# Scores of a cross-attention kernel: from 32-row tiles of TensorE to 64 x 64 tiles

## The chip, the cores and the metric

The kernel runs on one core of a Trainium2 chip. The metric is the device time of one execution, in microseconds (us). The engines have short names in the profile: PE is TensorE's matmuls, PEld its weight loads, DVE is VectorE, ACT is ScalarE, POOL is GpSimd and SP is SyncE, which issues most DMAs.

## What is computed

The reference is a cross-attention with a second, small attention beside it, all in float32 (16 batches, 100 queries of 640, 718 keys of 384, 8 heads of 80):

```python
query = hidden_states @ Wq
keyt = enc @ Wk
valt = enc @ Wv
hs = _mha(query, keyt, valt)          # softmax(q k^T / sqrt(80)) v, 8 heads
ca_q1 = jnp.einsum('btc,th->bch', ca, Wq_ca)
ca_q1 = ca_q1[:, indices, :]
ca_hs1 = _mha(ca_q1, residual, residual)
ca_q2 = ca_hs1 @ Wq
ca_hs2 = _mha(ca_q2, ca @ Wk_ca, ca @ Wv_ca)
out = (hs + ca_hs2) @ Wout + b_out + residual
```

The change is about the product of queries and keys in the first `_mha`: for each batch and head, 718 keys by 100 queries, over 80 rows (the head's width).

## The kernel before

The 718 keys of a batch are cut into six chunks of 120 or 119 (`KC`, `KN` = 120). Scores are computed with the keys on the output's partitions: the stationary operand is a piece of the keys `kT` (head rows by 120 keys), the moving operand a piece of the queries `qp` or `qz` (head rows by 100 queries). Exponentials `st` then serve as stationary operand of the weighted values (L1419), whose outputs are 64 and 36 queries on two column tiles.

A head has 80 rows, which do not divide the 128 rows of TensorE's array. The kernel permutes the columns of `Wq` and `Wk` so that each head's first 64 rows lie in chunks 0 to 3 of `kT` and `qp`, and the last 16 rows of all eight heads together in chunk 4 (`qz` for the queries). Before the change the first 64 rows of a head stand as two halves of 32 rows, in the same quarter of the partitions, in two chunks. So `scores` issues for each key chunk four matmuls for each of five row chunks, one in each group of 32 rows (`RG` = 4), and these four write to four banks. A head's score is the sum of two halves and of the last 16 rows. In chunk 4 a group of 32 rows holds two heads; `qz` keeps the queries of each with the other's rows masked, so these matmuls stream 200 columns instead of 100.

A batch has three groups (`g` = 0, 1, 2) of two key chunks each. `scores(b, g, tiles)` issues 40 matmuls in four banks of PSUM, and ScalarE copies them to `st`: in two copies (L629) for groups 0 and 2, which share the double-bank pool `ps2`, in four copies (L623) for group 1, which takes its banks from `psk` and `ps1`. The eight banks are all in use, so group 2 waits for the copies of group 0.

The batches follow each other in an order written out by hand (`tc.manual_schedule`, from L1199): three groups of scores, softmax2 of the second attention (`z_ps`, L788, four column tiles), its next products (`y_ps`, L736), then the products that make the next batch's keys and this batch's values (L432, L463, L557) while DVE, ScalarE and GpSimd work on the softmax, then the weighted values (`a_ps`, L1419), and the next batch. Every second batch also computes the queries of the next two batches (`q_ps`, L533). In front of the loop the weights are loaded and permuted: `load_packed` (L69) loads the transposed Wk, in nine DMAs of SP's queue, and DVE copies Wq into its permuted place (L1148 and L1155).

Of the kernel before, what the change touches and what calls it, by code (L numbers as in the profile page):

```python
# [14 lines left out]
B, S, H = 16, 100, 640  # L15
NH, D = 8, 80
CAD, T = 384, 4
SK = 722 - T
P = 128
HC = H // P  # L20
# [3 lines left out]
KN = KT // 2  # L24

KC = [(u, j) for j in range(2) for u in range(3)]
# [27 lines left out]
for h in range(NH):  # L54
    lo = h * D
    while lo < (h + 1) * D:
        c = lo // P
        hi = min((h + 1) * D, (c + 1) * P)
        PIECES.append((h, c, lo - h * D, lo - c * P, hi - lo))
        lo = hi  # L60
# [5 lines left out]
RG = 4  # L66


def load_packed(load, to, w):  # L69

    rows = w.rearrange("(r u k) n -> r u k n", r=RG, u=2)
    for r, u in [(r, u) for r in range(RG) for u in range(2)]:
        load(
            out=to[32 * r : 32 * r + 32, 2 * u : 2 * u + 2],
            in_=rows[r, u, :64].rearrange("(j p) n -> p j n", j=2),
        )
    load(out=to[:, 4], in_=w.rearrange("(h k) n -> h k n", h=NH)[:, 64:])

# [45 lines left out]
def kernel(  # L126
# [18 lines left out]
    nc = tc.nc  # L145
# [14 lines left out]
    def pair(name):  # L160
        tile = ps2.tile([P, 2, 512], F32, tag="ps2", name=name)
        return tile
# [21 lines left out]
    def scores_tile(name):  # L184
        return main.tile([P, 2, ROWS], F32, tag="st", name=name, bufs=NP)
# [28 lines left out]
    def load_enc(b):  # L214
        enc = enc_tile(f"enc_{b}"), None
        for u, lo, hi in ((0, 0, 3), (1, 1, 3), (2, 0, 2)):
            at = A_RAW[u, lo]
            nc.sync.dma_start(
                out=enc[0][:, at : at + hi - lo],
                in_=enct[b][:, lo:hi, u * (KT - 1) : u * (KT - 1) + KT],  # L220
            )
        return enc

    def load_rest(b, enc):
        if b == 1:
            room = hsT_tile("rest_1").rearrange("p c s -> p (c s)")
            rest = room[:, : len(A_REST) * KT].rearrange("p (i k) -> p i k", k=KT)
        else:
            rest = rest_tile(f"rest_{b}")
        for (u, c), i in A_REST.items():  # L230
            nc.sync.dma_start(
                out=rest[:, i], in_=enct[b][:, c, u * (KT - 1) : u * (KT - 1) + KT]
            )
        return enc[0], rest
# [6 lines left out]
    def a_form(enc, f):  # L241
        return enc[0][:, A_AT[f]]
# [10 lines left out]
    wq_sb = const.tile([P, HC, H], F32, name="wq_sb")  # L253
    kT = const.tile([P, HC, 3, KT], F32, name="kT")
# [22 lines left out]
    for g in range(2):  # L277
        for c in range(CC):
            nc.scalar.dma_start(
                out=wv_sb[:, 2 * c + g],  # L280
                in_=wv[c * P : (c + 1) * P, g * (H // 2) : (g + 1) * (H // 2)],
# [15 lines left out]
    ca_0 = small.tile([S, T, S], F32, tag="ca", name="ca_0")  # L297
    in_order(nc.sync.dma_start(out=ca_0, in_=cas[0].unsqueeze(0).to_broadcast([S, T, S])))
    load_packed(
        lambda **ends: in_order(nc.sync.dma_start(**ends)), wkt_sb[:, :, :CAD], wkt  # L300
    )
    halves = [t[:, u] for t in [scores_tile(f"wq_{i}") for i in range(NP)] for u in range(2)]
    room = halves.pop()
    wq_in = [t[:, :H] for t in halves]
# [19 lines left out]
    for h, c, r, s, k in PIECES:  # L324
        nc.gpsimd.dma_start(
            out=m2[s : s + k, c, h - HEADS[c][0], :T],
            in_=wqcat[h * D + r : h * D + r + k, :],
# [4 lines left out]
    for c in range(HC):  # L332
        first = c * P - HEADS[c][0] * D
        nc.gpsimd.affine_select(
            out=hmask[:, c], in_=hmask[:, c], compare_op=ALU.is_ge, fill=0.0,
# [3 lines left out]
            out=hmask[:, c], in_=hmask[:, c], compare_op=ALU.is_ge, fill=0.0,  # L339
# [68 lines left out]
    class Values(Blocks):  # L408
# [17 lines left out]
        def product(self, at, f, first, last):  # L426
            for bank in "AB":
                if self.opened[bank] is at and bank in self.fresh:
                    first = True
                    self.fresh.discard(bank)  # L430
            for j in range(2):
                nc.tensor.matmul(  # L432
                    at[0][j][:KN, : H // 2],
                    a_form(self.enc, f)[:, j * KN : (j + 1) * KN],
                    wv_there.get(f, wv_sb[:, W_AT[f]]),
                    start=first,
                    stop=last,
                    skip_group_check=True,
                )
# [152 lines left out]
    def scores(b, g, tiles):  # L592

        qp, qz = tiles
        name = f"s_ps_{b}_{g}"
        if g == 1:
            s_ps = [f(f"{name}_{r}") for r, f in enumerate((psumk, psumk, psum1, psum1))]
        else:
            pairs = [pair(f"{name}_{i}") for i in range(2)]
            s_ps = [pairs[r // 2][:, r % 2] for r in range(RG)]  # L600
        n = KN
        for a in range(2):
            u, j = KC[2 * g + a]
            for c in range(HC):
                for r in range(RG):
                    rows = slice(32 * r, 32 * r + 32)
                    if c < 4:
                        rhs = qp[rows, c // 2, c % 2, (b % 2) * S : (b % 2 + 1) * S]
                        lo, hi = (c // 2) * S, (c // 2 + 1) * S
                    else:  # L610
                        rhs, lo, hi = qz[rows, 0, b % 2], 0, 2 * S
                    nc.tensor.matmul(  # L612
                        s_ps[r][:n, 256 * a + lo : 256 * a + hi],
                        kT[rows, c, u, j * KN : (j + 1) * KN],
                        rhs,
                        start=(a == 0 and c == 0),
                        stop=(c == HC - 1),
                        skip_group_check=True,
                    )
        st = scores_tile(f"st_{b}_{g}")[:n]  # L620
        if g == 1:
            for r in range(RG):
                nc.scalar.copy(  # L623
                    st[:, :, 2 * r * S : 2 * (r + 1) * S],
                    s_ps[r][:n].rearrange("p (a q) -> p a q", a=2)[:, :, : 2 * S],
                )
        else:
            for i in range(2):
                nc.scalar.copy(  # L629
                    st[:, :, 4 * i * S : 4 * (i + 1) * S].rearrange(  # L630
                        "p a (r q) -> p r a q", r=2
                    ),
                    pairs[i][:n].rearrange("p r (a q) -> p r a q", a=2)[:, :, :, : 2 * S],
                )
        return st
# [80 lines left out]
    class Second:  # L716
# [87 lines left out]
        def load(self):  # L804
            self.vb = [self.piece(nc.gpsimd, t) for t in range(2)]
# [282 lines left out]
    for n in range(HC):  # L1088
        for c in range(CC):
            for lo in (0, 64):  # L1090
# [4 lines left out]
                    start=(c == 0),  # L1095
                    stop=(c == CC - 1),
                )
    k2T, at = [], 0
    for n, heads in enumerate(HEADS):
        cols = len(heads) * B * T  # L1100
# [10 lines left out]
    for c in range(HC):  # L1111
        m_ps = psum(f"m_ps_{c}")
        for n, heads in enumerate(HEADS):
# [4 lines left out]
                start=(n == 0),  # L1118
                stop=(n == HC - 1),
                skip_group_check=True,  # L1120
# [23 lines left out]

    with tc.issue_after(summed.ins):
        for c in range(HC):
            for u in range(2):
                nc.vector.tensor_copy(  # L1148
                    wq_sb[:, c, 2 * u * P : 2 * (u + 1) * P].rearrange(
                        "p (a r k) -> p a r k", a=2, r=RG  # L1150
                    ),
                    wq_in[c].rearrange("p (r k) -> p r k", r=RG)[:, :, u * D : u * D + 64]
                    .rearrange("p r (a k) -> p a r k", a=2),
                )
            nc.vector.tensor_copy(  # L1155
                wq_sb[:, c, 4 * P :].rearrange("p (h k) -> p h k", h=NH),
                wq_in[c].rearrange("p (h k) -> p h k", h=NH)[:, :, 64:],
            )
# [7 lines left out]
    for c in range(CC):  # L1166
        for n in range(2):
# [4 lines left out]
                start=(c == 0),  # L1172
                stop=(c == CC - 1),
# [3 lines left out]
    for n in range(2):  # L1177
        nc.scalar.dma_start(
            out=va_d[:, n * (H // 2) : (n + 1) * (H // 2)],
            in_=va[n * B * T : (n + 1) * B * T],  # L1180
# [10 lines left out]
    last, enc_next, second_next = None, load_rest(1, load_enc(1)), Second(1, xT)  # L1191
# [8 lines left out]
    for b in range(B):  # L1200
        p = b // 2
# [37 lines left out]
        if b == 0:  # L1239
            enc_sums(enc)  # L1240
            now.load()
            now.softmax1()
        st.append(scores(b, 0, tiles))
        if b == 0:
            now.exponentials1()
        nc.vector.tensor_tensor(most[:KN], st[0][:, 0], st[0][:, 1], ALU.max)
        st.append(scores(b, 1, tiles))
        larger(1)
        st.append(scores(b, 2, tiles))

        now.softmax2()
# [39 lines left out]
        elif b + 1 < B:  # L1291
# [68 lines left out]
            if last.b in PAIRS:  # L1360
                second.softmax1(3)
                last.project_pair()
                if last.b == max(PAIRS):
                    nc.sync.dma_start(
                        out=forms[1],
                        in_=wout[: 2 * P, H // 2 :].rearrange("(c p) n -> p c n", p=P),
# [40 lines left out]
        for g in range(2):  # L1407
# [6 lines left out]
            for h, i in order:  # L1414
# [3 lines left out]
                for lo, hi in QC:  # L1418
# [4 lines left out]
                        start=(i == 0 and h in (0, *range(4, NH))),  # L1423
                        stop=(i == len(KC) - 1),
                        skip_group_check=True,
# [6 lines left out]
            cols = slice(4 * g * D, 4 * (g + 1) * D)  # L1432
# [11 lines left out]
        last = mine  # L1444
# [55 lines left out]
```

## Time and profile before

| | |
|---|---|
| median of 3 runs | 930.88 us |
| lowest, highest | 930.83, 931.11 us |
| span of the profiled execution | 929.5 us |
| instructions in the profile | 25894 |
| PE, PEld busy | 922.4 (99%), 787.6 (85%) us |
| DVE, ACT, POOL busy | 693.2 (75%), 433.9 (47%), 678.2 (73%) us |
| granted TensorE clock | 1.000 |

The span runs from the first to the last instruction of the profiled execution. No own time of that execution is given beside its span; the timed runs are 1.3 to 1.6 us longer than it. PE and PEld overlap: the array streams one tile's columns while the next weights are loaded. A float32 matmul stands as two records on PE and two on PEld. The records' durations are latencies of single instructions, and several tiles of the array can be at work at once, so a group's pitch is read from starts and not from durations.

### The profile page before, as it was taken

To read this page: it belongs to the slowest core of one execution; us is meant where nothing else is said; L and a number is where in the kernel's file an instruction comes from. 1 tells how busy PE (TensorE), PEld (TensorE's weight loads), DVE (VectorE), ACT (ScalarE), POOL (GpSimd) and SP (SyncE) were. 2 spreads that over 40 slices of the span, in tenths; PEclk is the share of its full clock that TensorE was granted. 3 is DMA by queue.
4 is the path that set the end of the run, shared out by engine and by line. 5 is a ranking of instruction groups with operands and counts; after the bars stand their busy time and mean duration, and the time that the engine had idled before them with its cause. 6 is when DMAs were issued, how large, how long until landed. Compare 5 with 4: busy or idle time off the path is not lost.

```text
span 929.5 us, 25894 instructions
## 1 busy us (share of the span) xinstructions
PE 922.4 (99%) x11130; PEld 787.6 (85%) x11130; DVE 693.2 (75%) x1085; ACT 433.9 (47%) x836; POOL 678.2 (73%) x646
## 2 busy tenths in 40 slices
PE   9999999999999999999999999999999999999998
PEld 6998989797897979888798788988879888797966
DVE  3859895989739896685967869579873888838884
ACT  2234543736337363652726436264641737427341
POOL 5757998788938877496884968758895578956724
PEclk9999999999999999999999999999999999999999
DMA  8722022040300304031030400205030050310201
GB/s 262 264 85 77 25 66 76 7 149 2 117 17 23 105 13 120 2 103 53 28 105 3 120 36 30 75 2 154 2 103 30 2 154 2 102 45 2 82 19 41
DMA packets 49673, 62.82 MB, mean 68 GB/s; under 512 B 14072, under 2 KB 38200, under 8 KB 49560
## 3 DMA queue, kind: packets, MB, share of 16 engines
q1 hardware_dynamic: 45512, 51.49, 18.3%
q0 software_dynamic: 3024, 8.53, 3.0%
q8 instruction: 87, 1.43, 0.6%
q10 hardware_dynamic: 1024, 1.15, 0.4%
q14 instruction: 26, 0.21, 0.1%
HBM read 55.59 MB, written 5.57 MB: 66 GB/s over the span
## 4 chain that ended last, share of the span: by engine, by line
PE 97%; DVE 2%; DMA 0%; issue 0%; ACT 0%; POOL 0%; ACTq 0%; DVEq 0%
PE s_ps L612 12%; PE a_ps L1419 12%; PE v_psA L432 11%; PE v_psB L432 9%; PE kT_ps L557 8%; PE k_psA L463 7%; PE q_ps L533 7%; PE k_psB L463 6%; PE o_ps L1013 5%; PE v_psC L432 3%; PE k_psC L463 3%; PE v_psD L432 2%; PE v_psE L432 2%; PE y_ps L736 2%; PE v_ps L373 1%; PE k_psE L463 1%
## 5 line engine op out<-in xcount | busy, mean ns | idle before, releaser
L761 POOL TENSOR_TENSOR e<-ca,g 100x800 f32<-100x800 f32 x64 | 99.4, 1564 | 126.8 <-DVE most L1234 99.7
L498 POOL TENSOR_TENSOR enc<-enc 128x240 f32<-128x240 f32 x135 | 106.7, 800 | 19.7 <-DMA enc<-in_enct 12.7
L1222 DVE TENSOR_TENSOR st<-st,over 120x1600 f32<-120x1600 f32 x48 | 117.0, 2439 | 0.0
L1419 PEld LDWEIGHTS a_ps<-vs,st 120*36 120x36 f32 (+3 forms) x3072 | 109.3, 125 | 5.9 <-issue 5.8
L1419 PE MATMUL a_ps<-vs,st 120*36 120x81 f32 (+3 forms) x3072 | 112.2, 233 | 0.9 <-issue 0.9
L432 PE MATMUL v_psA<-wv_sb,enc 128*120 128x320 f32 x352 | 109.8, 434 | 0.0
L862 POOL TENSOR_TENSOR hs<-hs,hs 100x640 f32<-100x640 f32 x48 | 100.5, 2095 | 3.8
L612 PE MATMUL s_ps<-qp,kT 32*120 32x100 f32 x3072 | 97.5, 263 | 0.0
L855 POOL TENSOR_TENSOR hs<-vb,p 100x640 f32<-100x640 f32 x64 | 89.6, 1411 | 9.5 <-issue 4.7
L612 PEld LDWEIGHTS s_ps<-qp,kT 32*120 32x120 f32 x3072 | 94.7, 179 | 1.7 <-issue 0.2
L629 ACT COPY st<-s_ps 120x800 f32<-120x800 f32 x64 | 49.7, 828 | 98.1 <-PE s_ps L612 98.1
L768 POOL TENSOR_TENSOR e<-e,e 100x800 f32<-100x800 f32 x48 | 92.0, 1917 | 3.8
L432 PE MATMUL v_psB<-wv_sb,enc 128*120 128x320 f32 x296 | 91.8, 433 | 0.0
L1230 ACT ACTIVATE st<-st 120x1600 f32<-120x1600 f32 x48 | 73.9, 1539 | 32.3 <-DVE st L1222 32.1
L463 PE MATMUL k_psA<-enc,wk_sb 128*128 128x240 f32 x360 | 87.7, 366 | 0.0
L1234 DVE TENSOR_TENSOR most<-most,st 120x800 f32<-120x800 f32 x64 | 69.0, 1078 | 21.9 <-ACT st L623 20.8
L463 PEld LDWEIGHTS k_psA<-enc,wk_sb 128*128 128x128 f32 x360 | 68.3, 190 | 16.7
L432 PEld LDWEIGHTS v_psA<-wv_sb,enc 128*120 128x120 f32 x352 | 63.2, 183 | 22.6 <-DVE vs L403 0.5
L463 PE MATMUL k_psB<-enc,wk_sb 128*128 128x240 f32 x300 | 73.1, 366 | 0.1
L432 PEld LDWEIGHTS v_psB<-wv_sb,enc 128*120 128x120 f32 x296 | 54.1, 183 | 21.9 <-DVE vs L403 0.4
L928 ACT COPY hsT<-turned_hs 32x160 f32<-32x160 f32 (+7 forms) x244 | 67.7, 278 | 3.0
L533 PE MATMUL q_ps<-xT,wq_sb 128*128 128x200 f32 x400 | 69.1, 333 | 0.0
(168 smaller groups left out, 1802.9 us busy)
## 6 DMA issues: line engine op xcount, KB each, us to landing
vb<-va_d POOLq DMA_DIRECT2D x32, 250.0 KB, 3.5
vb<-va_d SPq DMA_DIRECT2D x32, 250.0 KB
enc<-in_enct SPq DMA_DIRECT2D x30, 240.0 KB
enc<-in_enct SPq DMA_DIRECT2D x15, 360.0 KB
xT<-in_xt SPq DMA_DIRECT2D x8, 500.0 KB
rest<-in_enct SPq DMA_DIRECT2D x31, 120.0 KB
xn<-in_x SPq DMA_DIRECT2D x11, 320.0 KB
out<-xn SPq DMA_DIRECT2D x11, 320.0 KB
```

Of the source, the lines that this page charges most:

```text
L432: nc.tensor.matmul(at[0][j][:KN, : H // 2], a_form(self.enc, f)[:, j * KN : (j + 1) * KN], wv_there.get(f, wv_sb[:, W_AT[f]]), start=first ...
L463: nc.tensor.matmul(at[:, i * KT : (i + 1) * KT], wk_sb[:, W_AT[f], i], a_form(self.enc, f), start=(first and i == 0), stop=last, skip_grou ...
L498: nc.gpsimd.tensor_tensor(out, left, right, op)
L533: nc.tensor.matmul(q_ps[:, : 2 * S].rearrange("p (j s) -> p j s", j=2), wq_sb[:, c, n * P : (n + 1) * P], xT[:, :, c, :], start=(c == 0), ...
L557: nc.tensor.matmul(bank[:, i * KT : (i + 1) * KT], weights[c], a_raw(enc, u, c), start=(i == 0 and c == 0), stop=(c == CC - 1), skip_group ...
L612: nc.tensor.matmul(s_ps[r][:n, 256 * a + lo : 256 * a + hi], kT[rows, c, u, j * KN : (j + 1) * KN], rhs, start=(a == 0 and c == 0), stop=( ...
L761: first = nc.gpsimd.tensor_tensor(to, self.ca[:, t, :].unsqueeze(1).to_broadcast([S, NH, S]), g[:, :, t].unsqueeze(2).to_broadcast([S, NH, ...
L768: nc.gpsimd.tensor_tensor(e, e, to, ALU.add)
L855: first = nc.gpsimd.tensor_tensor(to, self.vb[t][:S].rearrange("p (h d) -> p h d", h=NH), p2[:, :, t].unsqueeze(2).to_broadcast([S, NH, D] ...
L862: nc.gpsimd.tensor_tensor(sums, sums, to, ALU.add)
L1222: return nc.vector.tensor_tensor(st[i], st[i], top.over[:KN].unsqueeze(1).to_broadcast([KN, 2, ROWS]), ALU.subtract,)
L1419: nc.tensor.matmul(a_v[lo:hi, h % 4], st[i // 2][: KEYS[i], i % 2, h * S + lo : h * S + hi], block(i, h // 4)[: KEYS[i], h % 4], start=(i ...
```

## The change

The first 64 rows of a head now lie together, in one half of the partitions: heads 0 to 3 in rows 0 to 63 of chunks 0 to 3, heads 4 to 7 in rows 64 to 127. Their scores are computed in tiles of 64 rows by 64 columns: the 120 keys of a chunk are cut in two column tiles of 64 and 56 keys (`KH`). Four such matmuls (two halves of rows, two column tiles) take the place of the four in groups of 32 rows, with the same 100 columns streamed and the same number of matmuls, 32 in a group. The last 16 rows stay in four groups of 32 rows, 120 keys wide, 200 columns streamed, 8 matmuls in a group. They are no longer issued after each key chunk: a group issues the first rows of both chunks and then the last rows of both, and group 1 the other way round. The permutation of Wq (DVE) and the load of the transposed Wk (nine DMAs, as before) follow the new places.

```diff
+KH = [(0, 64), (64, KN)]
 def load_packed(load, to, w):
-    rows = w.rearrange("(r u k) n -> r u k n", r=RG, u=2)
-    for r, u in [(r, u) for r in range(RG) for u in range(2)]:
-        load(
-            out=to[32 * r : 32 * r + 32, 2 * u : 2 * u + 2],
-            in_=rows[r, u, :64].rearrange("(j p) n -> p j n", j=2),
-        )
-    load(out=to[:, 4], in_=w.rearrange("(h k) n -> h k n", h=NH)[:, 64:])
+    rows = w.rearrange("(h k) n -> h k n", h=NH)
+    for h in range(NH):
+        r, c = divmod(h, RG)
+        load(out=to[64 * r : 64 * r + 64, c], in_=rows[h, :64])
+    load(out=to[:, 4], in_=rows[:, 64:])
...
         n = KN
-        for a in range(2):
-            u, j = KC[2 * g + a]
-            for c in range(HC):
+        begun = set()
+        def product(at, part, w, rhs, cols, last):
+            k0, k1 = part
+            nc.tensor.matmul(
+                s_ps[at][k0:k1, cols],
+                w,
+                rhs,
+                start=not begun & {(at, k) for k in range(k0, k1, 32)},
+                stop=last,
+                skip_group_check=True,
+            )
+            begun.update((at, k) for k in range(k0, k1, 32))
+        def first_rows(last):
+            for a in range(2):
+                u, j = KC[2 * g + a]
+                for c in range(RG):
+                    rhs = qp[:, c // 2, c % 2, (b % 2) * S : (b % 2 + 1) * S]
+                    for r in range(2):
+                        h, rows = RG * r + c, slice(64 * r, 64 * r + 64)
+                        lo = 256 * a + (h % 2) * S
+                        for k0, k1 in KH:
+                            product(
+                                h // 2,
+                                (k0, k1),
+                                kT[rows, c, u, j * KN + k0 : j * KN + k1],
+                                rhs[rows],
+                                slice(lo, lo + S),
+                                last,
+                            )
+        def last_rows(last):
+            for a in range(2):
+                u, j = KC[2 * g + a]
                 for r in range(RG):
                     rows = slice(32 * r, 32 * r + 32)
-                    if c < 4:
-                        rhs = qp[rows, c // 2, c % 2, (b % 2) * S : (b % 2 + 1) * S]
-                        lo, hi = (c // 2) * S, (c // 2 + 1) * S
-                    else:
-                        rhs, lo, hi = qz[rows, 0, b % 2], 0, 2 * S
-                    nc.tensor.matmul(
-                        s_ps[r][:n, 256 * a + lo : 256 * a + hi],
-                        kT[rows, c, u, j * KN : (j + 1) * KN],
-                        rhs,
-                        start=(a == 0 and c == 0),
-                        stop=(c == HC - 1),
-                        skip_group_check=True,
+                    product(
+                        r,
+                        (0, n),
+                        kT[rows, 4, u, j * KN : (j + 1) * KN],
+                        qz[rows, 0, b % 2],
+                        slice(256 * a, 256 * a + 2 * S),
+                        last,
                     )
+        steps = (last_rows, first_rows) if g == 1 else (first_rows, last_rows)
+        for i, step in enumerate(steps):
+            step(i == 1)
...
         for c in range(HC):
-            for u in range(2):
+            for r in range(2):
                 nc.vector.tensor_copy(
-                    wq_sb[:, c, 2 * u * P : 2 * (u + 1) * P].rearrange(
-                        "p (a r k) -> p a r k", a=2, r=RG
-                    ),
-                    wq_in[c].rearrange("p (r k) -> p r k", r=RG)[:, :, u * D : u * D + 64]
-                    .rearrange("p r (a k) -> p a r k", a=2),
+                    wq_sb[:, c, : 4 * P].rearrange("p (n r k) -> p n r k", n=RG, r=2)[
+                        :, :, r
+                    ],
+                    wq_in[c].rearrange("p (r n k) -> p r n k", r=2, n=RG)[:, r, :, :64],
                 )
```

## The prediction

> **What bounds the kernel now.** I read the page first (engines, then the chain that ended last), then the list of waits of the weight loads, then the scores line by itself, then the TensorE timeline through one batch.
>
> ```profile
> span 929.5 us, 25894 instructions
> PE 922.4 (99%) x11130; PEld 787.6 (85%) x11130; DVE 693.2 (75%) x1085; ACT 433.9 (47%) x836; POOL 678.2 (73%) x646
> ...
> PE 97%; DVE 2%; DMA 0%; issue 0%; ACT 0%; POOL 0%; ACTq 0%; DVEq 0%
> PE s_ps L612 12%; PE a_ps L1419 12%; PE v_psA L432 11%; PE v_psB L432 9%; PE kT_ps L557 8%; PE k_psA L463 7%; PE q_ps L533 7%; PE k_psB L463 6%; PE o_ps L1013 5%; PE v_psC L432 3%; PE k_psC L463 3%; PE v_psD L432 2%; PE v_psE L432 2%; PE y_ps L736 2%; PE v_ps L373 1%; PE k_psE L463 1%
> ```
>
> TensorE carries 97% of the chain and is never idle for long; DVE, the next, has a quarter of the span free. What shortens TensorE's own work therefore shortens the run, as long as nothing else comes late. The scores are 12% of the chain, about 112 us, all on the path.
>
> The span is 929.5 us, the median of the runs 930.88: 1.4 us lie around the span. I work out the change of the span and take it off the median.
>
> Now the scores by themselves, and below them the weighted values (L1419), softmax2 (L788) and a value product (L432). Columns: engine, operation, out<-in, count, duration in ns (min/median/max), first and last start in us, forms; the a_ps matmuls are those of one batch, and the a_ps weight load is a row of the groups by shape (busy us, mean ns, idle before).
>
> ```profile
> L612 PEld LDWEIGHTS s_ps<-qp,kT x3072: 174/180/180, 60.0 to 885.6; 32*120 32x120 f32 x192
> L612 PE MATMUL s_ps<-qp,kT x3072: 244/263/342, 60.0 to 885.7; 32*120 32x100 f32 x192
> L612 PEld LDWEIGHTS s_ps<-qz,kT x768: 174/180/180, 60.9 to 885.8; 32*120 32x120 f32 x192
> L612 PE MATMUL s_ps<-qz,kT x768: 327/338/413, 60.9 to 886.0; 32*120 32x200 f32 x192
> L612 PEldq EVENT_SEMAPHORE  x38: 51/51/51, 98.0 to 881.0; - x38
> ...
> L1419 PE MATMUL a_ps<-vs,st x192: 231/233/284, 310.6 to 317.3; 120*64 120x81 f32 x64, 120*36 120x81 f32 x64, 119*36 119x81 f32 x32, 119*64 119x81 f32 x32
> ...
> L1419 PEld LDWEIGHTS a_ps<-vs,st 120*64 120x64 f32 x1024 | 84.5, 136 | 5.9 <-issue 5.8
> ...
> L788 PEld LDWEIGHTS z_ps<-y_sb,e x1024: 82/109/113, 67.3 to 886.8; 100*32 100x32 f32 x113, 100*4 100x4 f32 x58
> L788 PE MATMUL z_ps<-y_sb,e x1024: 191/195/218, 67.4 to 886.8; 100*32 100x33 f32 x105, 100*4 100x33 f32 x66
> ```
>
> [...] Four row groups run side by side, so four records make one set. Two prices come out of the durations:
> - **Streaming.** 200 columns take 327 ns at best, 100 take 244: 83 ns per 100 columns, 0.83 ns a column.
> - **Loading weights.** 120 columns take 180 ns, 4 columns 82 (the z row's minimum): 98 / 116 = 0.84 ns a column. So 120 columns need 100 ns, 64 need 54.
>
> The median 100-column matmul takes 263 ns, 19 more than the best one: it waits for weights, since its set streams in 83 ns while the next set's weights need 100. So 100-column sets are bound by the weight load, 200-column sets (167 ns of streaming) by the stream. The timeline of batch 5 gives the pitch (start us, duration us, engine, line, what, records):
>
> ```profile
> 310.55 6.99 PE L1419 MATMUL a_ps<-vs,st 120*64 120x81 f32 x192
> 317.47 1.10 PE L612 MATMUL s_ps<-qp,kT 32*120 32x100 f32 x32
> 318.39 0.54 PE L612 MATMUL s_ps<-qz,kT 32*120 32x200 f32 x8
> 318.75 1.00 PE L612 MATMUL s_ps<-qp,kT 32*120 32x100 f32 x32
> 319.57 0.54 PE L612 MATMUL s_ps<-qz,kT 32*120 32x200 f32 x8
> 319.92 1.00 PE L612 MATMUL s_ps<-qp,kT 32*120 32x100 f32 x32
> ...
> 322.28 1.00 PE L612 MATMUL s_ps<-qp,kT 32*120 32x100 f32 x32
> ...
> 323.46 1.00 PE L612 MATMUL s_ps<-qp,kT 32*120 32x100 f32 x32
> 324.28 0.54 PE L612 MATMUL s_ps<-qz,kT 32*120 32x200 f32 x8
> 324.75 0.75 PE L788 MATMUL z_ps<-y_sb,e 100*32 100x33 f32 x64
> 325.42 0.31 PE L736 MATMUL y_ps<-m,xT 128*100 128x72 f32 x1
> ```
>
> A half group (one key chunk) takes (323.46 - 318.75) / 4 = 1.178 us: eight sets of 100 columns and two of 200. A stream-bound product shows what a set costs beyond its streaming:
>
> ```profile
> 293.61 1.24 PE L432 MATMUL v_psC<-wv_sb,enc 128*120 128x320 f32 x4
> 294.68 1.24 PE L432 MATMUL v_psA<-wv_sb,enc 128*120 128x320 f32 x4
> ```
>
> Four records in 1.07 us are 268 to 269 ns each for 320 columns, where 0.833 x 320 = 266.7: about 2 ns more. So two 200-column sets take 2 x 169 = 338 ns, and a 100-column set (1178 - 338) / 8 = **105 ns**. A stream-bound one would take 83.3 + 2.5 = **86 ns**.
>
> **The 64-row tiles.** The new sets hold two row groups of 64 and two key column tiles of 64 and 56; still four records to a set, 100 columns streamed, 8 x 2 sets a group, 48 groups: 768 sets. Only the weight load changes, from 120 columns to 64 in the widest tile: 54 ns, under the stream. The pitch becomes 86 ns if the two column tiles of a row group load and stream side by side. No row shows two row groups and two column tiles at once. The bounds are from the nearest rows: a_ps has two column tiles of 64 and 36 over all rows and 81 columns streamed: 192 records, 96 pairs, between 310.55 and 317.47, so 6.92 / 96 = 72 ns a pair with both ends in it, against 67.5 + 2.5 of stream alone. Were their loads one after the other, 100 columns would need 84 ns. And z loads four column tiles (3 x 32 + 4 columns): 64 records, 16 sets, in 0.67 us (324.75 to 325.42, where y_ps starts), 42 ns a set, half of what 100 columns in a row need. So I take 86 ns, near a_ps: 768 x 19 ns = **14.6 us gained**. The pitch cannot go under the stream, 83 ns; the upper bound is 105 if loads queue, and the cases beyond are rivals.
>
> [...]
>
> **The switches of tile shape.** Before, a batch enters the 32-row tiles once (from a_ps or q_ps) and leaves once (to z_ps). After, the order is group 0 first rows, last rows; group 1 last rows, first rows; group 2 first rows, last rows: the last rows of groups 0 and 1 and the first rows of 1 and 2 adjoin. That makes three shape changes more in each of 16 batches. Their price: the two 200-column sets take 0.35 us from 319.57 to 319.92, where scores follow, and 0.47 from 324.28 to 324.75, where z follows, which has another shape: **0.11 us** in which the array runs empty. On top, the first weights are not hidden: the longest 100-column matmul takes 342 ns, 98 more than the best (120 columns), the longest a_ps matmul 284, 51 more than the median (64 columns). So into 32 x 120: 0.21 us; into 64 x 64: 0.16 us.
> - Added: two changes to last rows, 0.42; one back to first rows, 0.16. The entry loads 64 columns in place of 120: -0.05. Sum 0.53 us a batch, 16 batches: **8.5 us lost**.
> - Bounds: with z's small load (218 - 195 = 23 ns), the cheapest change seen costs 0.13, three of them 0.40, 5.6 us with the entry. The dearest by rows is 0.21 for each, 9.3 us.
>
> **Other edits.** Last rows keep shape, 200 columns and count: 0. The weight shuffle on DVE keeps ten copies of 256 elements:
>
> ```profile
> L1148 DVE COPY wq_sb<-wq x10: 281/288/1961, 30.2 to 35.3; 128x256 f32<-128x256 f32 x10
> ...
> L533 PE MATMUL q_ps<-xT,wq_sb x50: 332/333/437, 51.4 to 59.7; 128*128 128x200 f32 x50
> ```
>
> They end 14 us before their reader, which covers them; without cover they would cost some 3 us once. The load of Wk's transpose keeps nine DMAs on SP's queue, with as many rows of the same length; nothing moves past them: 0. In the built program z_ps waits for one more event, group 1's matmuls on its own engine, over 2 us old by then; a wait record is 51 ns in a sequencer that runs ahead: 0.
>
> **What is late next.** Group 2 reuses the banks of group 0, which ScalarE must have copied out:
>
> ```profile
> 320.19 1.55 ACT L629 COPY st<-s_ps 120x800 f32<-120x800 f32 x2 [3.51 <-PE s_ps L612]
> ```
>
> The copies end at 321.74, 1.82 us after group 0's last set (319.92). Group 1 shrinks from 2.36 us (322.28 - 319.92) to 4 x 0.169 + 16 x 0.086 + 0.16 = 2.21. The margin falls from 0.54 to 0.39 us: still free. Group 1's first copies can start four sets earlier, off the path.
>
> **Sum.** A batch now: 0.10 + 48 x 0.105 + 12 x 0.169 + 0.11 = 7.28 us, which is 317.47 to 324.75. After: loads 0.05 + 0.10 + 0.05 + 0.10, four times 0.11, 48 x 0.086, 12 x 0.169: 6.90. That is 0.38 us a batch, 6.1 us in all: span 923.4, time **924.8 us**.
>
> **Rivals.**
> 1. *The shape changes cost more than the sets save* (slower). It decides above (14.6 + 0.8) / 48 = 0.32 us a change; the dearest priced above is 0.21, but none of those goes between two row-tiled shapes. At 0.45 each: 48 x 0.26 = 12.5 us more, 937. Chance 0.03.
> 2. *A tile's load waits for matmuls in its row group*: sets of 86 + 54 = 140 ns, 768 x 35 = 27 us, with 8.5 for the switches 966. Against it: a_ps at 72 ns. Chance 0.04.
> 3. *The loads of the two column tiles of a row group queue*: 64 + 56 = 120 columns, so 105 ns as before; the gain is nothing and the entry's 0.8 goes too: about 940. Against it: a_ps and z. Chance 0.04.
> 4. *Two of the four tiles take turns streaming*: 172 ns a set, 51 us, with the switches 991. Nothing for it but that the mixture is not in the trace. Chance 0.03.
> 5. *No change*: sets near 94 ns, or switches near 0.32. Time 929 to 932.7. Chance 0.06.
>
> **How the numbers follow.** Forecast 0.80: sets 86 to 90 ns (0 to +3 us), switches 0.13 to 0.25 each (-3 to +3 us), and something below for a change that drains less than any seen. That gives 921 to 930; with the case of no change up to 930.5 and 0.5 below, the range is 920.5 to 930.5. A measurement of this kernel tells 0.2%, 1.9 us, from no change; faster means under 929.0. Slower is the sum of rivals 1 to 4.
>
> **What would show it.** After: the 64 x 64 matmuls' median within a few ns of their minimum (no wait for weights), weight loads near a_ps's 136 ns (64 columns) instead of 180, last rows unchanged, and z_ps starting 6.9 us after the first scores record instead of 7.28, in every batch. A median 19 ns or more above the minimum, or first and last rows more than 0.21 us apart at their borders, would make the steps wrong; a wait of s_ps on ScalarE would show that the banks come free too late.

## Result, and the profile after

| | before | after |
|---|---|---|
| median, four runs each on one chip | 930.86 us | 925.56 us |
| lowest, highest | 930.26, 931.11 us | 925.19, 926.35 us |
| span of the profiled execution | 929.5 us | 923.5 us |
| PE busy | 922.4 us | 916.1 us |
| PEld busy | 787.6 us | 773.0 us |

The ratio is 0.9946, with a 95% interval from 0.9931 to 0.996: the changed kernel is faster by 5.3 us. The forecast was 924.8 us, in a range from 920.5 to 930.5. The changed kernel ran twice more, beside the kernel before on those chips: 927.34 (ratio 0.9958, 0.9943 to 0.9973) and 927.32 us (0.9955, 0.9941 to 0.9968). So the gain was 5.3, 3.9 and 4.2 us in the three sets. The profiled execution took 925.19 us.

The page of the changed kernel: the span, the engines, and the chain that ended last by engine and by line.

```profile
span 923.5 us, 25899 instructions
PE 916.1 (99%) x11130; PEld 773.0 (84%) x11130; DVE 687.4 (74%) x1085; ACT 434.0 (47%) x836; POOL 685.2 (74%) x646
...
PE 96%; DVE 2%; DMA 0%; issue 0%; ACT 0%; POOL 0%; ACTq 0%; DVEq 0%
PE a_ps L1453 12%; PE s_ps L608 11%; PE v_psA L433 11%; PE v_psB L433 9%; PE kT_ps L558 8%; PE k_psA L464 8%; PE q_ps L534 7%; PE k_psB L464 6%; PE o_ps L1048 5%; PE v_psC L433 3%; PE k_psC L464 3%; PE v_psD L433 2%; PE v_psE L433 2%; PE y_ps L771 2%; PE v_ps L374 1%; PE k_psE L464 1%
```

TensorE still carries the chain (96%), with as many matmul records as before (x11130). The scores have gone from 12% to 11%.

The scores line by itself (engine, operation, out<-in, count, shortest/median/longest in ns, first and last start in us, forms):

```profile
L608 PEld LDWEIGHTS s_ps<-qp,kT x3072: 123/128/134, 60.1 to 879.0; 64*64 64x64 f32 x183, 64*56 64x56 f32 x9
L608 PE MATMUL s_ps<-qp,kT x3072: 246/246/298, 60.1 to 879.1; 64*64 64x100 f32 x183, 64*56 64x100 f32 x9
L608 PEld LDWEIGHTS s_ps<-qz,kT x768: 174/178/178, 61.6 to 879.8; 32*120 32x120 f32 x192
L608 PE MATMUL s_ps<-qz,kT x768: 327/328/425, 61.6 to 879.9; 32*120 32x200 f32 x192
```

The 100-column matmul now has its median at its minimum, 246 ns (before: 263 over 244). The 19 ns of waiting for weights are gone; the weight loads of the new tiles take 128 ns in place of 180. The longest matmuls stand at the borders: 298 - 246 = 52 ns into 64 x 64, 425 - 328 = 97 ns into 32 x 120. The prediction had 51 and 98 from other rows.

The TensorE timeline of batch 5 (start us, duration us, engine, line, what, records):

```profile
310.14 6.99 PE L1453 MATMUL a_ps<-vs,st 120*64 120x81 f32 x192
317.06 1.60 PE L608 MATMUL s_ps<-qp,kT 64*64 64x100 f32 x64
318.59 1.63 PE L608 MATMUL s_ps<-qz,kT 32*120 32x200 f32 x32
320.15 2.97 PE L608 MATMUL s_ps<-qp,kT 64*64 64x100 f32 x128
323.05 0.95 PE L608 MATMUL s_ps<-qz,kT 32*120 32x200 f32 x16
323.93 0.75 PE L823 MATMUL z_ps<-y_sb,e 100*32 100x33 f32 x64
```

The differences of the starts can be held against the prediction's sum, block by block. A block is its first load, its sets, and the 0.11 us of empty array behind it:

| block | from the prediction's numbers | measured |
|---|---|---|
| 16 sets of 64 x 64 | 0.05 + 16 x 0.086 + 0.11 = 1.54 | 318.59 - 317.06 = 1.53 |
| 8 sets of last rows | 0.10 + 8 x 0.169 + 0.11 = 1.56 | 320.15 - 318.59 = 1.56 |
| 32 sets of 64 x 64 | 0.05 + 32 x 0.086 + 0.11 = 2.91 | 323.05 - 320.15 = 2.90 |
| 4 sets of last rows | 0.10 + 4 x 0.169 + 0.11 = 0.89 | 323.93 - 323.05 = 0.88 |

Together 6.87 us from the first scores to `z_ps`, where 6.90 was said and 7.28 was before. The blocks also separate the pitch from the price of a border: 16 sets more, with the same borders, take 2.90 - 1.53 = 1.37 us, 86 ns a set. The median batch takes 6.872 us for the scores, where it took 7.276: 16 x 0.404 = 6.46 us less per execution.

**Where the rest of the 6.0 us of span is.** The other intervals between batches do not all stay. In batch 0 the time from the first `z_ps` to the first `a_ps` grew from 24.39 to 26.13 us, 1.74 lost (before, then after):

```profile
67.35 0.75 PE L788 MATMUL z_ps<-y_sb,e 100*32 100x33 f32 x64
...
91.75 2.47 PE L1419 MATMUL a_ps<-vs,st 120*64 120x81 f32 x64
```

```profile
66.93 0.75 PE L823 MATMUL z_ps<-y_sb,e 100*32 100x33 f32 x64
...
93.06 1.12 PE L1453 MATMUL a_ps<-vs,st 120*64 120x81 f32 x26
```

On the other side the profiled execution of the kernel before had an idle stretch in batch 12 (the interval between two batches' scores 48.97 us, where after it is 47.50, that is 1.06 more than the 0.4 of the scores) that the profile names only "issue"; the experiment on column tiles shows it to be a wait for instructions. In the list of waits of that kernel it is this row:

```profile
PE a_ps L1419 <- issue: 0.9, 1, 0.9
```

6.46 - 1.74 + 1.06 = 5.8; the last 0.2 us is spread over small differences.

The loss in batch 0, in the waits of TensorE's matmuls of the changed kernel (who waits, for whom, us in all, times, longest):

```profile
PE idle_ps L1114 <- DVE idle L1111: 1.1, 1, 1.1
PE k_psA L464 <- DVE kT L404: 1.1, 1, 1.1
PE y_ps L771 <- POOL m L744: 0.5, 1, 0.5
PE m_ps L1149 <- issue: 0.5, 1, 0.5
PE k_psB L464 <- DVE sm L873: 0.3, 1, 0.3
```

The second and the last row were not there before. No row names ScalarE: the banks of group 0 come free in time, as the prediction had it. VectorE's `kT` sums are late because of what stands ahead of them on VectorE, the maximum of group 2, two operations. First the kernel before, then the changed one, from the timelines of VectorE and GpSimd:

```profile
69.93 3.23 DVE L1234 TENSOR_TENSOR most<-most,st 120x800 f32<-120x800 f32 x2
70.15 4.41 POOL L761 TENSOR_TENSOR e<-ca,g 100x800 f32<-100x800 f32 x2 [0.56 <-issue]
```

```profile
69.49 4.97 DVE L1268 TENSOR_TENSOR most<-most,st 120x800 f32<-120x800 f32 x2
70.56 3.04 POOL L796 TENSOR_TENSOR e<-ca,g 100x800 f32<-100x800 f32 x2
```

And the duration of one such operation over the whole execution (shortest/median/longest ns), `most` before and after and GpSimd's product after:

```profile
L1234 DVE TENSOR_TENSOR most<-most,st x64: 981/992/2212, 66.8 to 889.3; 120x800 f32<-120x800 f32 x64
```

```profile
L1268 DVE TENSOR_TENSOR most<-most,st x64: 981/992/3956, 66.5 to 883.0; 120x800 f32<-120x800 f32 x64
L796 POOL TENSOR_TENSOR e<-ca,g x64: 1534/1539/1552, 35.5 to 845.6; 100x800 f32<-100x800 f32 x64
```

Alone `most` takes 0.99 us. Before, the longest took 2212 ns, some 1.2 more; after, 3956 ns, nearly two GpSimd products (2 x 1539) more. So it looks as if VectorE's operation stood still while GpSimd ran one product before, and two after. That was a reading of one trace; the last experiment tests it.

### The profile page after: what moved, and what is told of

Its sections match the earlier page's. It is cut to its first block, busy times and chain, and to the rows that moved or that the text cites. A ratio compares the mean times of both kernels' runs of the same rounds, so it can differ in the third digit from the quotient of the medians.

```text
span 923.5 us, 25899 instructions
## 1 busy us (share of the span) xinstructions
PE 916.1 (99%) x11130; PEld 773.0 (84%) x11130; DVE 687.4 (74%) x1085; ACT 434.0 (47%) x836; POOL 685.2 (74%) x646
## 3 DMA queue, kind: packets, MB, share of 16 engines
q8 instruction: 87, 1.43, 0.6%
## 4 chain that ended last, share of the span: by engine, by line
PE 96%; DVE 2%; DMA 0%; issue 0%; ACT 0%; POOL 0%; ACTq 0%; DVEq 0%
PE a_ps L1453 12%; PE s_ps L608 11%; PE v_psA L433 11%; PE v_psB L433 9%; PE kT_ps L558 8%; PE k_psA L464 8%; PE q_ps L534 7%; PE k_psB L464 6%; PE o_ps L1048 5%; PE v_psC L433 3%; PE k_psC L464 3%; PE v_psD L433 2%; PE v_psE L433 2%; PE y_ps L771 2%; PE v_ps L374 1%; PE k_psE L464 1%
## 5 line engine op out<-in xcount | busy, mean ns | idle before, releaser
L499 POOL TENSOR_TENSOR enc<-enc 128x240 f32<-128x240 f32 x135 | 111.0, 832 | 16.5 <-DMA enc<-in_enct 9.4
L1268 DVE TENSOR_TENSOR most<-most,st 120x800 f32<-120x800 f32 x64 | 71.2, 1113 | 15.6 <-ACT st L658 14.4
L608 PE MATMUL s_ps<-qp,kT 64*56 64x100 f32 (+1 forms) x3072 | 73.1, 248 | 0.0
L608 PEld LDWEIGHTS s_ps<-qp,kT 64*56 64x56 f32 (+1 forms) x3072 | 66.9, 130 | 5.6 <-issue 4.2
```

Of the source, the lines that this page charges most:

```text
L499: nc.gpsimd.tensor_tensor(out, left, right, op)
L608: nc.tensor.matmul(s_ps[at][k0:k1, cols], w, rhs, start=not begun & {(at, k) for k in range(k0, k1, 32)}, stop=last, skip_group_check=True,)
```

## Experiments

**The changed kernel again.** It ran in two other sets of runs, beside experiments.

> The changed kernel once more, to see whether batch 0's late products (26.1 us from z_ps to a_ps in batch 0, where the kernel before had 24.4) come again. Theory (VectorE and GpSimd collide there by the program's own timing): 26.1 us again and 925 to 926 us. Rival (chance of one execution): 24.0 to 24.6 us in batch 0, and about 924 us.

> The changed kernel, unchanged, on the same chip as the two others: 925.2 to 927.5 us, and 26.1 us from z to the weighted values in batch 0.

927.34 and 927.32 us, spans 925.7 and 925.6; the scores last 6.87 us again, in 14 and 13 of the 16 batches. Batch 0 shows 26.14 and 26.28 us from z to the weighted values: its loss is the program's own and no accident of one execution. The first time is above the 925 to 926 us expected. Its profiled execution has two idle stretches of TensorE around batch 5 that are named only "issue", and the two intervals they stand in are 1.8 us longer than in the first execution; the second run has two such stretches as well. They are of the kind that the experiment on column tiles explains.

**The price of a shape change.** The same tiles, but the last rows issued after each key chunk, so that eleven shape changes stand in a batch's scores instead of three:

```diff
-        steps = (last_rows, first_rows) if g == 1 else (first_rows, last_rows)
-        for i, step in enumerate(steps):
-            step(i == 1)
+        for a in range(2):
+            first_rows(False, [a])
+            last_rows(True, [a])
```

> The changed kernel, but the last rows are issued after each key chunk, as before the change: twelve runs of tile shapes a batch instead of four, so 11 shape changes inside a batch instead of 3. Theory (a change of shape costs 0.10 to 0.11 us of empty array plus the first weight load, 0.10 us for 120 columns and 0.05 for 64): four more changes to last rows at 0.20 and four more back at 0.16 are 1.44 us a batch, 23 us in all: about 948.6 us. Rival (the array does not run empty between two row-tiled shapes, the set pitch alone made the difference): 925 to 927 us. Rival (order does not matter but the banks come free too late): a wait of s_ps on ScalarE and a time in between.

Measured 947.04 us (946.93 to 948.5), ratio 1.0173 (1.0158 to 1.0188). The TensorE timeline of one batch, to the start of z:

```profile
322.66 0.91 PE L608 MATMUL s_ps<-qp,kT 64*64 64x100 f32 x32
323.50 0.61 PE L608 MATMUL s_ps<-qz,kT 32*120 32x200 f32 x8
324.05 0.91 PE L608 MATMUL s_ps<-qp,kT 64*64 64x100 f32 x32
...
331.04 0.75 PE L823 MATMUL z_ps<-y_sb,e 100*32 100x33 f32 x64
```

The first rows of a chunk hold 323.50 - 322.66 = 0.84 us (0.05 + 8 x 0.086 + 0.11 = 0.85), the last rows 0.55 (0.10 + 2 x 0.169 + 0.11 = 0.55). In the batches without other waits (the one shown has a short one) the scores last 8.315 us, 1.44 more than in the changed kernel: eight changes at 0.18 us each, which is the mean of the prediction's 0.21 and 0.16. The time is 1.6 us under the 948.6 expected; batch 0 does not lose its time here (24.03 us from z to the weighted values). In this order the 64-row tiles lose 16 us against the kernel before. The price of a change decides the sign, and the grouping of the steps is what pays for the tiles.

**One column tile.** The 64-row tiles with all 120 keys in one load:

```diff
-KH = [(0, 64), (64, KN)]
+KH = [(0, KN)]
```

> The changed kernel with all 120 keys in one column tile (64 rows by 120 keys; half as many matmuls for the first rows, two in a set). Theory (the gain comes from the narrower weight load): a set needs 100 ns for its weights again, pitch 105 ns instead of 86, 768 sets, and two entries a batch load 120 columns instead of 64: 14.6 + 1.5 us more than the changed kernel, about 941.5 us, slower than before the change. Rival (the gain comes from one matmul of 64 rows in place of two of 32, or from the order): 925 to 926 us.

Measured 939.13 us (938.95 to 939.97), ratio 1.0084 (1.0067 to 1.0101). The scores line, weight loads and matmuls of the first rows:

```profile
L608 PEld LDWEIGHTS s_ps<-qp,kT x1536: 176/182/182, 60.0 to 893.9; 64*120 64x120 f32 x192
L608 PE MATMUL s_ps<-qp,kT x1536: 265/265/343, 60.0 to 893.9; 64*120 64x100 f32 x192
```

The load is 182 ns again, the matmul's median 265: the 19 ns are back, with two tiles to a set and half as many loads. So with 120 columns to load, the pitch of a set is the load's, with 64 rows as with 32. The scores last 7.83 us, 0.96 longer than in the changed kernel (1.0 expected, from 48 sets at 105 instead of 86 ns and two longer first loads). The time is 2.4 us under the 941.5 expected, and again batch 0 takes 24.03 us from z to the weighted values. This is also what rival 3, loads in a queue, would have made of the change: 940 was said, 939 it is here.

**The order alone.** The old 32-row tiles, with the steps in the new order:

> The kernel before with the order of the change alone: first rows of both key chunks, then last rows of both, group 1 the other way round; tiles of 32 rows by 120 keys as before. Theory: sets cost 105 and 169 ns wherever they stand, so no change, 930 to 931.5 us. Rival (part of the gain is the order's, for example that group 1's banks are copied earlier): 925 to 929 us.

```diff
-        for a in range(2):
+        firsts = [(a, c) for a in range(2) for c in range(HC - 1)]
+        lasts = [(a, HC - 1) for a in range(2)]
+        steps = lasts + firsts if g == 1 else firsts + lasts
+        for i, (a, c) in enumerate(steps):
...
```

Measured 931.22 us (930.43 to 933.34), ratio 1.0005 (0.9996 to 1.0014); the scores last 7.276 us as before. The order by itself brings nothing; its part is to keep the shape changes few.

**Column tiles without the change of shape.** If the load bounds the 32-row tiles, two column tiles of 64 and 56 keys in the old tiles should bring the 86 ns and need no inner shape change:

```diff
-                    nc.tensor.matmul(
-                        s_ps[r][:n, 256 * a + lo : 256 * a + hi],
-                        kT[rows, c, u, j * KN : (j + 1) * KN],
...
+                    for k0, k1 in ((0, 64), (64, KN)):
+                        nc.tensor.matmul(
+                            s_ps[r][k0:k1, 256 * a + lo : 256 * a + hi],
+                            kT[rows, c, u, j * KN + k0 : j * KN + k1],
...
```

> The kernel before with one edit: every scores matmul is cut in two column tiles of 64 and 56 keys, rows in four groups of 32 as before, so eight tiles in a set, one shape for first and last rows, no change of shape inside the scores, and twice as many matmuls (80 a group). Theory (weight load of 64 columns hides under the 86 ns stream, shape changes eat 8.5 us of the change's gain): sets at 86 ns, no inner change, entry load 0.05 us shorter: 14.6 + 0.8 us less than before, about 915.5 us, ahead of both kernels. Rival (eight tiles a set are bound by the issue of 16 loads and matmuls, some 7 ns each): 112 ns a set of 100 columns, 936 us or more. Rival (loads in one row group queue): 105 ns, 930 us.

A miss: 1042.23 us (1037.9 to 1048.13), ratio 1.1196 (1.1149 to 1.1243). First lines from the list of waits of the weight loads, then the page's instruction queue (packets, MB, share) in this run and in the kernel before, then the timeline of one batch:

```profile
PEld s_ps L613 <- issue: 67.9, 46, 2.2
PEld z_ps L789 <- issue: 21.1, 25, 3.1
```

```profile
span 1036.2 us, 33574 instructions
...
q8 instruction: 117, 1.92, 0.8%
```

```profile
span 929.5 us, 25894 instructions
...
q8 instruction: 87, 1.43, 0.6%
```

```profile
357.37 0.77 PE L613 MATMUL s_ps<-qp,kT 32*64 32x100 f32 x39 [1.27 <-issue]
...
361.38 0.54 PE L613 MATMUL s_ps<-qz,kT 32*64 32x200 f32 x6 [1.81 <-issue]
```

Each batch's scores stand still for one to two microseconds several times, for nothing that another engine does. The kernel has 33574 - 25894 = 7680 instructions more, four for each of the 1920 added matmuls, and the queue moves 1.92 - 1.43 MB = 0.49 MB more, 64 bytes an instruction. Between the two gaps above lie 128 matmul records, 64 matmuls, 256 instructions: 16,384 bytes, which is the size of each packet of that queue in the trace. While scores run, such packets start 3.4 to 4.3 us apart, 3.7 in the middle (in one batch at 300.46, 304.12, 308.14, 312.16 and 316.09 us). So 64 matmuls per 3.7 us, 58 ns a matmul, is about what TensorE is given here; a batch of 240 scores matmuls is 3.75 packets, some 14 us, and takes 10.6 to 13.9, so part of it seems to be there already.

The packets can be held against the stalls. From the first scores on, TensorE stands still 60 times in this run for more than 0.3 us with nothing named but "issue", 79.5 us in all, and each time it goes on 1.20 to 1.55 us after one of these packets has landed: the two gaps above end at 357.37 and 361.38 us, the packets landed at 355.88 and 359.94. Matmuls at large do not keep that distance; in the changed kernel most scores matmuls start anywhere from 0.3 to 4.0 us after the last landing. So these are waits for instructions, and they make up 79.5 of the 106.7 us by which the span is longer. A further part is the granted TensorE clock: nine times it stands at 0.50 for 3.4 us, as from 361.5 to 364.9 us, which would be some 15 us (9 x 3.4 x 0.5) if TensorE is the limit throughout them. In the profiles of the kernel before and of the changed one it does not fall before the last microseconds.

Two runs test that reading. The first cuts only group 0 of the 32-row tiles, 160 matmuls in a batch:

> The kernel before with the column split of the fourth experiment in group 0 alone (32 rows by 64 and 56 keys, eight tiles a set, 80 matmuls in group 0); groups 1 and 2 as before, so 160 matmuls a batch instead of 120 or 240, and two shape changes a batch... one inner change, to 120 columns, 0.20 us. Theory A (the full split was slow because instructions arrive too slowly: 16 KB, 64 float matmuls, in 3.5 to 4 us): the instructions that are already fetched cover group 0, its 100-column sets of eight run at 86 ns and group 0 lasts 0.05 + 16 x 0.086 + 4 x 0.169, 2.1 us, followed by a stall later in the scores or none; no stall inside group 0. Theory B (eight tiles of 32 x 64 do not stream side by side): group 0's sets take 167 ns from the first on and it lasts 3.5 us or more.

One execution, 949.68 us. From the timeline, first the cut group and then the gap:

```profile
323.09 0.99 PE L613 MATMUL s_ps<-qp,kT 32*64 32x100 f32 x60
...
325.60 1.10 PE L613 MATMUL s_ps<-qp,kT 32*120 32x100 f32 x32
...
327.79 0.77 PE L613 MATMUL s_ps<-qp,kT 32*120 32x100 f32 x18 [0.34 <-issue]
```

The cut group 0 runs without a stall and lasts 325.60 - 323.09 = 2.51 us here; the stall comes two microseconds later, in a group that is not cut. So it is in the other batches: one alone has a stall in the cut group, of 0.20 us, and all those over 0.3 us come behind it. A limit in the tiles would lie in the cut group. The gap shown ends 1.41 us after a packet has landed (326.38 us), and all 18 stalls of this run over 0.15 us end 1.26 to 1.57 us after one. But the tiles are no better without a stall: 2.51 us, with 0.16 for the first load and the border, for a group that takes two times 1.18 = 2.36 uncut, where 2.1 was expected; a set of eight tiles took some 100 to 105 ns on average, not 86. The starts of the single records show that 86 is possible: three sets follow each other at it (139, 225, 311 and 397 ns after the first record), and then come records of 286 to 293 ns, where the others take 244. So neither the dispatch of eight loads and eight matmuls nor the loads of two column tiles in one 32-row group holds back every set; what holds the longer ones these runs do not tell.

The second cuts the last rows of the changed kernel, 144 matmuls in a batch instead of 120:

```diff
-                    product(
-                        r,
-                        (0, n),
-                        kT[rows, 4, u, j * KN : (j + 1) * KN],
...
+                    for k0, k1 in KH:
+                        product(
+                            r,
+                            (k0, k1),
+                            kT[rows, 4, u, j * KN + k0 : j * KN + k1],
...
```

> The changed kernel with the last rows too in column tiles of 64 and 56 keys (32 x 64 tiles, eight a set, 200 columns): 48 matmuls a group instead of 40; the shape still changes three times inside a batch. Theory (the first weights of a shape are the unhidden part of a change): the two entries to the last rows load 64 columns instead of 120, 2 x 0.046 us a batch, 1.5 us less than the changed kernel, about 924 us. Rival (instruction supply, 64 float matmuls in 3.5 to 4 us, is already at its end with 120 matmuls in 6.9 us): 144 matmuls need 8 us and more, 16 to 30 us slower, with stalls that wait for nothing shown.

Measured 942.3 us (941.21 to 943.59), ratio 1.0119 (1.0102 to 1.0136), 15 us over the changed kernel on the same chip. The waits of its weight loads:

```profile
PEld s_ps L608 <- issue: 10.4, 28, 0.8
PEld z_ps L824 <- issue: 9.3, 22, 1.0
```

The rival was right in kind, and a little high in size: 15 us more, where it said 16 to 30, and 6.94 to 8.08 us for the scores, where it said 8 and more. All 19 idle stretches of TensorE over 0.15 us that are named "issue" end 1.23 to 1.58 us after a packet has landed. In the changed kernel a scores matmul comes every 6.87 / 120 = 57 ns, about the 58 ns of the supply above. It passes, as far as these runs tell, because what was fetched ahead covers a stretch of that length; 24 matmuls more in a batch already stall. It does not always pass: the idle stretch of the kernel before in batch 12 ends 1.48 us after a packet has landed, and those of the two repeats of the changed kernel 1.36 to 1.44 us after one.

**The loss in batch 0.** The changed kernel with one wait: GpSimd's first product for the next batch starts behind `most` of group 2. Then the same in the kernel before.

```diff
         if b == 0:
-            second.scores1()
+            second.scores1(seen)
```

> The changed kernel with one wait added: in batch 0 alone, the first product of GpSimd's scores1 for the next batch (L796) starts only behind the last of VectorE's `most` operations (L1268), as it does in other batches. Theory (collision): in batch 0 of the changed kernel those two `most` operations take 4.97 us instead of some 2 to 3.2, because two GpSimd products run in between, and that makes the kT sums late and TensorE wait 1.1 us, and more, for them; with the wait, `most` takes about 2.0 us, the time from z to the weighted values in batch 0 falls from 26.13 us to 24.0, and the kernel takes about 2 us less than the changed kernel: some 923.5 to 925. Rival (the loss comes from elsewhere, say the longer load or another engine's lateness): 26.1 us as before, and 925.5 to 927.5 as the changed kernel on the same chip. A second rival: GpSimd, 1 us later, makes something else late, and the time from z to the weighted values ends at 25 to 27 us.

> The kernel before with the same wait in batch 0. There `most` took 3.23 us, so the wait should bring little: from z to the weighted values in batch 0 24.39 us before, 24.0 to 24.4 expected, time within 0.5 us of the kernel before (930.4 to 931.4). If the wait by itself, and not the loss of the collision, were what helps, this kernel would gain as much as the changed one, about 2 us (929).

The changed kernel with the wait: 925.39 us (925.02 to 926.86), ratio 0.9937 (0.9925 to 0.995), beside 927.32 us for the changed kernel in the same set of runs. The kernel before with the wait: 931.13 us (929.81 to 932.41), ratio 0.9993 (0.9984 to 1.0002). The timelines of VectorE and GpSimd in the first:

```profile
70.03 2.01 DVE L1268 TENSOR_TENSOR most<-most,st 120x800 f32<-120x800 f32 x2
72.27 3.03 POOL L796 TENSOR_TENSOR e<-ca,g 100x800 f32<-100x800 f32 x2 [1.18 <-DVE most L1268]
```

`most` takes 2.01 us instead of 4.97, TensorE's waits for `kT` and `sm` are gone, and batch 0 takes 24.23 us from z to the weighted values instead of 26.28 in the changed kernel of that set (24.03 in the kernel before with the wait, 24.39 without). So the collision was the loss in batch 0, and the wait takes it away. The time is just above the 923.5 to 925 expected. It is the fastest version that ran, though its interval still touches that of the changed kernel; that the gain is the wait's is shown by batch 0, not by the times alone. With the collision out of both kernels the change is worth 931.13 - 925.39 = 5.7 us.

## Why the prediction was right

**The bound.** Right: TensorE's own work was the path, and 6.46 us less of it in the scores made the span 6.0 shorter.

**The pitch.** Right: 86 ns taken, and 86 ns measured between the blocks of 16 and of 32 sets. That the load of 120 columns and not the count of rows was the bound is shown by the run with one column tile. At rival 2's 140 ns a set the 32 sets of the third block would have taken 4.5 us, and they took 2.90 with their change of shape. Rivals 3 and 4, at 105 and 172 ns a set, are out by the same block.

**The shape changes.** Right in size: 0.21 and 0.16 us predicted, 0.18 on average measured by eight more of them. Rival 1 needed 0.32. The rows they came from were borders between other shapes.

**Edits priced at nothing.** Right: no wait on ScalarE, none of z's on the added event (its 51 ns records stand 0.84 to 0.86 us ahead of z's first load), and the first scores record starts at 60.1 us where it started at 60.0.

**What is late next.** Here a step was missing. The prediction asked it for ScalarE and the PSUM banks alone. VectorE's maximum of group 2 came 0.44 us earlier in batch 0 (69.49 instead of 69.93), GpSimd 0.41 us later (70.56 instead of 70.15). Before, GpSimd's first product started 0.22 us after the first of VectorE's two operations, and the engines took turns, one product between the two operations; after, it started 0.05 us behind the second operation, and both products went ahead of that one: 1.74 us. The other runs bear this out. With chunk order, one column tile or the order alone GpSimd started 0.21 to 0.22 us after the first operation, and batch 0 took 24.03, 24.03 and 24.61 us; in the two repeats and with the last rows cut it started 0.06 us behind the second, and batch 0 took 26.14, 26.28 and 25.95 us. That the forecast of the span was off by 0.1 us is therefore partly luck: it left out these 1.74 us, and it could not know that the profiled execution of the kernel before had lost 1.06 us to a wait for instructions and the changed one nothing. In the other two sets of runs, at 927.3 us and ratios of 0.9955 and 0.9958 against the 0.9935 forecast, it was some 2 us too low.

**One inference that the prediction did not need was wrong.** From its pitch it would follow that column tiles help the 32-row tiles as well. They made that kernel 111 us slower, mostly by waits for instructions, since a tile is four of them; and where no such wait stood, in the first cut group, the sets gained nothing either. The change itself keeps the count of matmuls, and so stays out of this.

## What to carry to other kernels

- Compare the median of a matmul group with its minimum: here a constant gap of 19 ns with short streams was the weight load, and a narrower column tile closed it where the number of matmuls stayed the same. Order the steps so that tiles of one shape adjoin; a shape change cost 0.18 us here, the gain of some nine sets.
- Before cutting matmuls finer, work out the time per matmul of the stretch. With 120 matmuls in 6.87 us, 57 ns each, the changed kernel had none to two idle stretches for want of instructions in each of three profiled executions; with 144 and 160 in a batch there were 19 and 18 over 0.15 us, and with 160 one alone stood in the group that was cut. An idle stretch named only "issue" can be held against the packets of the instruction queue.
- When an engine's step moves by half a microsecond, look at what runs beside it on VectorE and GpSimd: one operation's longest duration far over its median (3956 ns over 992) was such a collision here, and one wait in the right place took it away.

## What the runs showed of the hardware

- Column tiles of 64 and 56 in one group of 64 rows loaded and streamed beside each other at 86 ns a set of 100 float32 columns here, with two row groups at work.
- Leaving 64 x 64 for 32 x 120 tiles, or the other way, cost 0.18 us on average: 1.44 us for eight.
- TensorE's instructions came in packets of 16,384 bytes, 64 float32 matmuls, 3.4 to 4.3 us apart during the scores of the kernel that needed them fastest; a TensorE that had run out went on 1.20 to 1.58 us after a packet had landed.
- The granted TensorE clock stood at 0.50 for 3.4 us nine times in the kernel that waited for instructions most.
- A VectorE operation on two operands took 3956 ns instead of 992 while two GpSimd products ran; 2.01 us for two of them with GpSimd held back.
